# Graph attention, state-space mixer, relational layer and experts in one launch: mask transposes by transfer, small loads on another queue, and a new order of work

## The chip, the core and the metric

The kernel runs on one core of a Trainium2 chip. A core has five engines that run on their own and wait for each other through semaphores: PE (TensorE, matrix products and transposes into the PSUM banks), ACT (ScalarE), DVE (VectorE), POOL (GpSimd) and SP (SyncE, which issues transfers). Each engine executes its instructions in the order in which the program lists them; an instruction that waits holds up everything behind it on that engine. Transfers are issued from queues of SP, ACT and POOL and carried by 16 DMA engines that all queues share. SBUF is the working memory of 128 partitions, PSUM has eight banks of 128 x 512 floats, and the large tensors lie in the device's main memory (DRAM).

The metric is the device time of one launch in microseconds (us).

## The reference

`x` is 64 graphs of 256 nodes with 256 features in float32, `adj` the 64 adjacency matrices of 256 x 256 zeros and ones. Two layers follow one another, each of a graph part and a feed-forward part, each part with a residual and a layer norm (without scale) before it:

```python
x = x + _L0_gnn_ref(_layernorm(x), adj, W, a)                 # graph attention
x = x + _L0_ffn_ref(_layernorm(x), W_in, conv_w, ...)         # a Mamba-2 block
x = x + _L1_gnn_ref(_layernorm(x), ..., adj, weight, bias)    # relational layer
x = x + _L1_ffn_ref(_layernorm(x), gate_w, gate_b, w1, ...)   # 8 experts, top 1

def _L0_gnn_ref(h, adj, W, a):
    wh = einsum('bni,io->bno', h, W)
    s1, s2 = wh @ a[:Fout, 0], wh @ a[Fout:, 0]
    e = leaky_relu(s1[:, :, None] + s2[:, None, :], 0.2)
    e = where(adj > 0, e, NEG_BIG)
    return einsum('bmn,bno->bmo', softmax(e, axis=2), wh)

def _L1_gnn_ref(x, adj, relation, weight, bias):              # relation is adj
    masks = (relation[None] == rel_ids[:, None, None, None])  # 1..4
    h = einsum('rbnm,bmd->rbnd', masks, x)
    return einsum('rbnd,rdo->bno', h, weight) + bias
```

The Mamba-2 block projects to gates, values, B, C and dt, convolves over four positions, applies silu, mixes the 256 positions of a graph through a lower triangle of decays, gates, normalises by the root mean square and projects back (W_out, then W_lin). The expert layer sends each of the 16384 tokens to the expert with the largest gate, at most 2560 tokens to an expert, through relu(x w1 + b1) w2 + b2, scaled by the gate's probability.

## The kernel before

**Two passes.** The first pass (`first_pass`) goes through the 32 groups of two graphs (four tiles of 128 tokens each) and does everything up to the choice of an expert. It stores each token's row in a DRAM buffer (`x3d`) and its place in a list by experts (`slots`). The second pass (`second_pass`) goes through the blocks of 512 listed tokens (`wholes`) and of 128 (`quarters`): it gathers the rows, multiplies by the expert's weights and writes the rows out. Three whole blocks are already done within the first pass (`first_block`), to fill engines at its end, and the rows of the second pass's first block are fetched, normed and transposed there too (`lead`).

**The order of the first pass is planned.** Each function does not issue its instructions but registers steps with a planner (class `Plan`): engine, an assumed duration, what it reads and writes, an extra time until a result is visible (`late`), and the time of its transfer (`move`). `Plan.record` then simulates five engines and eight PSUM banks and issues the steps in the order in which they would begin; where several could begin at once, the one with the lower rank goes first. The rank is `PACE` times the group plus a due time from the tables `DUE` (a group's steps) and `LATE` (start and end). So the tables and the assumed durations set the order on every engine, and nothing else about the time: on the chip each engine follows its list and waits for what it needs. The second pass is not planned in this way; the framework orders its instructions.

**Start.** `prepare` loads and rearranges the weights. W_in goes to `win` (issued on ACT). `smaller` issues nine loads of small vectors, also from ACT: the convolution's weights `cw` and `cb` (halved on DVE afterwards), `aneg` (A_log), `dtb`, `dch` in two parts, `blin`, `brel`, `gb`. `centred` takes column means by a product with ones on PE (L516) and subtracts them on DVE (L522); `projected` transposes a matrix on PE (L533), copies it on ACT (L538) and multiplies it with the gate and logit columns (L544). The columns of W_in that give dt are copied on DVE out of `win` into the block `gq0` (L625). `aneg` becomes -exp(A_log) by an exponential on ACT (L638) and a product on DVE (L639), which wait for nothing but the load. `clear_slots` fills a tile on POOL and sends it over the `slots` list from ACT's queue (L721).

**A group.** `attention` loads x (L932) and the adjacency (`adji`, L935). ACT turns the adjacency into a bfloat16 mask `hide` (L947): 0 where an edge is, a large negative number elsewhere, three buffers. x is transposed on PE (L910) and copied by ACT (L915), multiplied with W (L871), and scaled by ACT into `wh` (L962). Then a chain begins: the logits `s2` are transposed on PE (L971), copied by ACT (`s2rows`, L973), written to DRAM and read back spread over all partitions by two transfers from SP (L975, L979); POOL adds the mask (`hm`, L983, two halves), ACT forms the other logits (`ev`, L989), DVE takes the row minima (L994), ACT the exponentials (L998), and PE transposes these (L1009) and multiplies them with `wh`. `scan` is the projection, the convolution (`y`, `xh`; DVE L1098, L1108) and the decays (four transfers `spread`, L1145; ACT `dm`, L1158 and L1164). `mix` multiplies decays and B-C products (DVE L1232, PE L1240 and L1244), gates and projects back. `relate` is the relational layer: products of the rows with the transposed mask `adjT`, then with the relation's weight. `choose`, once in two groups, finds experts and slots and scatters the token records (POOL L1436).

**The transposed masks.** In `mix`, for each of the two graphs of a group, PE transposes the four 128 x 128 blocks of `hide` with the bfloat16 identity `ident_b` into a PSUM bank (L1270), and ACT turns that into zeros and ones in `adjT` by a square with a scale and a bias (L1280), with a sum that is used to find adjacency values other than 0 and 1.

**Between the passes.** The second pass first fetches weights and token records, then gathers: `wholes.gather(0, None)` (rows of the first block, needed only as the residual there), then on POOL places and rows of `wholes` 1, `quarters` 0 and 1, then `quarters.norm(0)` on DVE.

Of the kernel before, what the change touches and what calls it, by code (L numbers as in the profile page):

```python
# [20 lines left out]
P = 128  # L21
# [15 lines left out]
    -26698, -26684, 16811, 5376, -1385, 22233, -9147, -5334, -6104, 16470, -4131, -12656,  # L37
    -16678, -3231, 6549, -17865, 6326, -26892, -31112, -17903, -11408, -796, -4422, -12203,
    -5594, 1406, -16327, -16058, -1084, -23798, -1397, -15584, 5401, -4898, -4435, 935, -15679,
    -4926, -36182, -30952, -7116, -5042, -13894, -12081, -3776, -29694, -776, -6149, -737,  # L40
    -14378, -1040, -15690, -8132, 2125, -13292, -19871, -13259, -19271, -17469, 3004, -3551,
    4598, 2717, -5807, -3518, -9626, -6760, -8973, -6760, -21580, -11090, -13187, -7075, -11614,
    8090, 12562, -15384, -25650, -16843, -17448, -16224, -33117, 17100, -11357, -1083, -673,
    -3047, -34625, -12261, -11942, 2714, -6609, 1789, 18383, -20000, 539, -3738, -33183, 333,
    14191, 6307, -9703, 30905, -7622, -19413, -14996, -28968, 116, 19317, 13445, 26060, -32817,
    248, -10405, 2927, -14690, 5944, -2080, -8721, 12774, 2204, -13729, 4024, -22409, -14504,
    5811, -7220, 1399, 13432, 6555, 4744, 7244, -13074, -17598, 12021, -2116, 1124, 383, 10928,
    4031, 2410, 19564, 20208, -4179, 14906, 17031, 1067, -9078, 28505, -6557, -15751, 31775,
    11208, -2943, -655, 18912, 7874, -12175, -12506, -31318, 19350, -32822, -27902, -1902,
    -2614, -22515, -11078, -32731, -7356, 9498, -25579, 6544, -6873, -12295, -8836, -15217,  # L50
    -101, -7100, 1503, -1212, -9384, -7250, 7131, 13184, 2367, 8234, -705, 2385, 15949, -10902,
    -6702, -11680, 4975, -8597, -19533, -14786, 2673, 6442, -7886, -3758, -14584, -18956, -2394,
    6472, -5117, -11835, -8654, 5355, -7098, 108, -26795, -19293, 8894, -21711, 8534, -22778,
    -5174, -16079, -18727, 6779, -14626, -18887, 15787, 204, 5445, -8225, -16055, 4780, 11196,
    -12432, -7396, 2489, -34797, 6092, -3614, -2035, -16485, -22244, -7928, 6163, -16171,
    -13402, 1393, 27308, -3299, 5434, 7440, -6001, 3226, -22066, 7952, -6124, -10687, 10110,
    -11601, -18846, 4084, -3318, -15991, -8790, -25459, 1833, -3473, -2961, -9107, -8293,
    -10502, -18974, -9710, -22513, -11406, -10557, -20206, -7421, -19897, -8699, -9302, -1570,
]
LATE = [  # L60
    -64053, -54702, -59145, -54915, -60062, -63895, -58481, -57817, -56638, -54542, -53887,
    -59553, -60544, -66295, -55138, -53590, -62371, -50547, -58476, -56411, -63929, -54771,
    -63020, -60249, -57757, -55870, -61971, -61584, -58713, -56315, -59515, -60412, -56997,
    -64050, -63593, -58710, -64327, -56974, -64548, -58677, -56261, -55764, -60770, -59294,
    -62214, -59216, -59275, -59000, -57674, -55104, -55629, -58061, -56012, -54911, -56448,
    -55347, -53242, -55651, -59000, -49001, -50233, -59769, -51850, -47995, -48427, -58143,
    -60315, -52513, -54188, -52953, -54782, -51621, -54327, -55185, -53707, -51746, -57084,
    -60544, -52244, -51134, -55346, -54169, -51215, -49728, -43803, -49582, -50567, -47711,
    -54575, -51840, -56142, -59770, -49885, 1346, -2673, -2320, -6355, -808, -6495, -5278,
    -5282, -4565, -4966, -834, -2200, -5069, -7821, -3201, -6160, -4309, -4527, -4910, -2257,  # L70
    -8341, -9201, -6505, -7591, -10768, -9145, -8325, -8954, 8280, 735, 3335, -7607, 7899, 6405,
    7444, -13853, 1045, -3011, 6416, -58, -9653, 9740, 2791, 9305, -3096, 1595, 7797, -2202,
    7339, -6677, 1395, 1189, 3316, 8270, 4320, 8345, 5395, -1209, 1024, 496, 4166, -5572, 10007,
    984, -7144, -1767, -9049, 430, 8168, 10157, 6125, 715, 2433, 5530, 2682, 9681, 4044, -3041,
    -2968, 5666, 3203, 7815, 2227, 4671, 4049, -972, 4835, -9096, 753, -943, -2244, 8804, -7176,
    9169, -3264, 14310, -351, -5008, 8557, -1420, 9011, 5402, 779, 9849, 8608, 3319, 8980, 5929,
    -754, -2251, 3474, -6957, 7127, 2274, 10247, -3481, 49, -3510, -403, -1726, 3946, 2006,
    -1802, 6377, 976, 1673, 5692, 3521, 6, -7831, -15890, 3058, 4170, -7076, 10709, 9000, 6424,
    5864, 2733, 2629, -4870, -702, -2673, 634, -1458, 1299, -687, 5733, -4310, 3394, -1918, 941,
    7852, -2182, 5064, -1684, 13692, 2798, 396, 8917, -2630, 8846, 9132, -2375, 11666, 11022,  # L80
    2337, 10279, 5111, 2075, -596, 5177, -3671, 3927, 3650, 11368, -4611, -3648, -135, -7000,
    2097, 4479, -1495, -2818, 6266, 3575, 372, 3192, -53, 1241, -9215, -13160, 8371, 1767,
    -8809, 9253, 10686, 2871, 6318, 5744, 6064, -7776, -3563, -2652,
# [59 lines left out]
class Plan:  # L143
# [6 lines left out]
    LEFT = 30  # L150

# [34 lines left out]
    def step(self, engine, us, go, reads, writes, late=0.0, port=0, move=0.0):  # L186
        k = self.k.get(self.due, 0)
        self.k[self.due] = k + 1
        due = (DUE if self.due == "group" else LATE)[k]
        step = Step(engine, us, go, self.g, self.TAIL[engine] + late, PACE * self.g + due,  # L190
# [128 lines left out]
def gnn_mamba_rgcn_moe(ctx: ExitStack, tc: tile.TileContext, a: dict, out: bass.AP):  # L319
# [33 lines left out]
    def row(ap):  # L353
        return ap.rearrange("(o d) -> o d", o=1)
# [33 lines left out]
    ident_b = const.tile([P, P], BF16, name="ident_b")  # L388
    nc.vector.tensor_copy(ident_b, ident)
# [92 lines left out]
    def first_pass(form, pass1):  # L482
# [80 lines left out]
        def smaller(s):  # L563

            def load(us, move, dst, src, home):
                s.step(ACT, us, lambda: nc.scalar.dma_start(out=dst, in_=src), [], [home], late=1.5, move=move)

            dskip = a["L0_ffn_D"].rearrange("(c q) -> q c", q=2)
            load(0.5, 0.2, cw, a["L0_ffn_conv_w"].rearrange("(c p) k -> p c k", p=P), s.fixed(cw))
            load(0.5, 0.2, cb, a["L0_ffn_conv_b"].rearrange("(c p) -> p c", p=P), s.fixed(cb))  # L570
            for half in (cw, cb):
                s.step(DVE, 0.1, lambda half=half: nc.vector.tensor_scalar(
                    half, half, 0.5, None, ALU.mult), [], [s.fixed(half)])
            load(0.5, 0.1, aneg, row(a["L0_ffn_A_log"]).broadcast_to([P, NH]), s.fixed(aneg))
            load(0.5, 0.1, dtb, row(a["L0_ffn_dt_bias"]).broadcast_to([P, NH]), s.fixed(dtb))
            for q in range(2):
                load(1.4, 0.1, dch[q * 64 : (q + 1) * 64, :], dskip[q : q + 1, :].broadcast_to([64, NCT]),
                     (s.fixed(dch), q))
            load(0.5, 0.5, blin[:, 0:D], row(a["L0_ffn_b_lin"]).broadcast_to([P, D]), (s.fixed(blin), "d"))
            load(0.5, 0.5, brel[:, 0:D], row(a["L1_gnn_bias"]).broadcast_to([P, D]), (s.fixed(brel), "d"))  # L580
            load(0.5, 0.1, gb, row(a["L1_ffn_gate_b"]).broadcast_to([P, E]), s.fixed(gb))

        def prepare(s):
# [36 lines left out]
            for i in range(2):  # L620
# [4 lines left out]
            s.step(DVE, 0.1, lambda: nc.vector.tensor_copy(gq0()[:, :, E + 1 :], win[:, :, DPROJ - NH :]),  # L625
                   [(win_, "dt")], [(two_, "q2")])
# [11 lines left out]
            s.step(ACT, 0.2, lambda: nc.scalar.activation(aneg, aneg, AF.Exp), [], [rate_])  # L638
# [78 lines left out]
        def clear_slots(s, homes):  # L717

            blank = s.tile("dm", [P, E * CAPP * 4 // P], bufs=4)
            s.step(POOL, 0.7, lambda: nc.gpsimd.memset(blank(), FAR), [], [blank])  # L720
            s.step(ACT, 0.5, lambda: nc.scalar.dma_start(  # L721
                out=slots.rearrange("(p j) w -> p (j w)", p=P), in_=blank()), [blank], homes, late=2.0, move=1.2)
# [457 lines left out]
        def mix(s, g, xe, entries, full, dt, gate, xh, bm, cm, dec):  # L1180
# [82 lines left out]
            adjT = []  # L1263
            for bi in range(2):
                ps, at = s.psum(BF16), s.tile("adjT", [P, 512], F32R, bufs=3)

                def turn(bi=bi, ps=ps):
                    for k in range(2):
                        for h in range(2):
                            nc.tensor.transpose(  # L1270
                                ps()[:, k * N + h * P : k * N + (h + 1) * P],
                                entries()[:, 2 * bi + h, k * P : (k + 1) * P],
                                ident_b,
                            )
# [349 lines left out]
    def second_pass(form, pass2):  # L1624
# [180 lines left out]
        for i in range(2):  # L1805
            quarters.fetch_weights(i)
# [76 lines left out]
```

## Time and profile before

| what | value |
|---|---|
| median of 3 runs | 2338.86 us (2333.72 to 2339.75) |
| profiled execution, its own time | 2332.68 us |
| its span, first to last instruction | 2331.0 us |
| granted PE clock, mean | 0.987 of full speed |
| instructions | 34861 |
| four mask transposes of a graph, count of instructions and busy time (L1270) | 256, 25.3 us |
| ACT's squares of the masks (L1280) | 64, 43.8 us |
| transfers of x and of adj, per group | 512 KB each, 5.3 and 4.6 us from issue to landing |
| transfers `spread`, four a group | 512 KB each, 4.0 us |

The profile is of one execution. Its span begins with the first instruction; the execution's own time is 1.7 us longer. Busy times of PE overlap, since products are pipelined: the busy time of a group of instructions can be more than what its absence would free. "PEld" is the loading of PE's weights, beside the products. Idle times are put down to what ended them ("<-"). Timeline lines show start, length, engine, line, operation, tiles written and read, and the idle time in front where there was some. In a table of stretches the columns are the stretch, its length, the busy time of PE, PEld, DVE, ACT and POOL with the number of instructions, the granted PE clock, the mean busy share of the DMA engines, and GB/s.

### The profile page before, as it was taken

Reading aid. Unit: us, or ns where it says so; the run is one execution under the profiler, and the core shown is the slowest. Engines: PE = TensorE matmul, PEld = TensorE weight load, DVE = VectorE, ACT = ScalarE, POOL = GpSimd, SP = SyncE. Lnnn points to the kernel's source line nnn. Section 1 sums busy time; section 2 is a strip of 40 time slices with the busy share of each in tenths; the row PEclk is TensorE's granted clock in tenths of the full one; section 3 lists DMA queues with packets and bytes.
Section 4 is the critical chain, followed back from the end, with each engine's and each line's share of the span. In section 5 each row is a group of like instructions: output and inputs, shape, how many; then the busy total and the mean of one; then the engine's idle time right before and its main releaser. Section 6 shows DMA issues by size and latency. Waiting matters only on the chain.

```text
span 2331.0 us, 34861 instructions
## 1 busy us (share of the span) xinstructions
PE 2232.1 (96%) x11079; PEld 1558.4 (67%) x11079; DVE 1757.0 (75%) x4396; ACT 1665.1 (71%) x3864; POOL 919.7 (39%) x994
## 2 busy tenths in 40 slices
PE   5999999999999999999999999999998999999996
PEld 4676766667676666766766667656665666666675
DVE  3899999999999998999998998799654434333342
ACT  3899999899999899999999988888632222222223
POOL 1233435354453445445354444533635222222221
PEclk7999999999999999999999999999999999999998
DMA  4333445444444445444444444424527333333336
GB/s 135 95 90 107 112 117 126 110 108 108 116 121 128 110 102 115 120 118 126 110 108 108 110 123 117 111 67 113 158 81 242 122 119 113 114 117 117 114 92 194
DMA packets 200022, 274.71 MB, mean 118 GB/s; under 512 B 28505, under 2 KB 165919, under 8 KB 199809
## 3 DMA queue, kind: packets, MB, share of 16 engines
q1 hardware_dynamic: 149968, 211.48, 28.9%
q0 software_dynamic: 46848, 58.91, 13.8%
q8 instruction: 93, 1.52, 0.3%
q10 hardware_dynamic: 2992, 1.81, 0.2%
q14 instruction: 121, 0.98, 0.2%
HBM read 187.70 MB, written 46.04 MB: 100 GB/s over the span
## 4 chain that ended last, share of the span: by engine, by line
PE 40%; issue 20%; ACT 12%; POOL 11%; DVE 10%; DMA 5%; SPq 0%; POOLq 0%; ACTq 0%; DVEq 0%
PE ps L871 26%; PE ps L1240 4%; POOL slots L1436 3%; POOL out_dram L477 3%; POOL xg L455 3%; ACT dm L1158 2%; DVE y L1098 2%; PE ps L910 2%; PE ps L1244 2%; PE ps L1543 1%; ACT dm L1164 1%; DMA x<-in_x_dram 1%; DVE dm L1232 1%; ACT xh L1256 1%; ACT xn L925 1%
## 5 line engine op out<-in xcount | busy, mean ns | idle before, releaser
L871 PE MATMUL ps<-xnT,win 128*128 128x512 f32 x1152 | 542.0, 597 | 4.8 <-ACT xnT L915 3.8
L1158 ACT ACTIVATE dm<-spread,cs 128x256 f32<-128x256 f32 (+1 forms) x1024 | 379.3, 452 | 22.6 <-PE ps L1244 22.6
L1098 DVE SCALAR_TENSOR_TENSOR y<-ps,cw,y 128x510 f32<-128x510 f32 (+2 forms) x480 | 351.5, 738 | 34.6 <-ACT y L1091 31.8
L871 PEld LDWEIGHTS ps<-xnT,win 128*128 128x128 f32 x1152 | 205.9, 190 | 171.6 <-issue 150.8
L1744 PE MATMUL ps<-w,hid 128*128 128x256 f32 x1184 | 263.3, 380 | 0.0
L871 PE MATMUL ps<-wf,gate 128*128 128x265 f32 x1024 | 250.8, 388 | 0.0
L1744 PEld LDWEIGHTS ps<-w,hid 128*128 128x128 f32 x1184 | 224.2, 191 | 37.0 <-issue 8.1
L1730 PE MATMUL ps<-xnT,w 128*128 128x512 f32 (+1 forms) x704 | 246.8, 509 | 1.5 <-ACT xnT L1711 1.5
L1232 DVE TENSOR_TENSOR dm<-dm,bc 128x1536 f32<-128x1536 f32 x128 | 225.2, 1760 | 2.5 <-ACT dm L1164 2.4
L871 PEld LDWEIGHTS ps<-wf,gate 128*128 128x128 f32 x1024 | 190.3, 190 | 45.2 <-issue 11.7
L1734 ACT ACTIVATE hid<-ps,b 128x512 f32<-128x512 f32 (+1 forms) x184 | 110.4, 604 | 129.4 <-PE ps L1730 126.1
L1730 PEld LDWEIGHTS ps<-xnT,w 128*128 128x128 f32 x704 | 120.6, 193 | 118.3 <-issue 111.0
L1164 ACT ACTIVATE dm<-dm 128x1536 f32<-128x1536 f32 x128 | 190.5, 1490 | 0.0
L1436 POOL DMA_INDIRECT slots<-meta,sl x128 | 153.8, 1201 | 50.6 <-issue 31.5
L1240 PE MATMUL ps<-dm,xdt 128*64 128x256 f32 x1024 | 169.4, 391 | 3.6 <-DVE xdt L1221 2.9
L889 DVE BATCH_NORM_STATS2 st<-x 128x6 f32<-128x256 f32 x384 | 155.2, 413 | 1.5 <-DMA x<-in_x_dram 1.3
L879 POOL TENSOR_SCALAR ve<-mv 128x4 f32<-128x4 f32 x96 | 36.6, 382 | 300.6 <-DVE mv L892 186.1
L1749 DVE SCALAR_TENSOR_TENSOR yv<-ps,meta,bp 128x256 f32<-128x256 f32 x50 | 24.2, 484 | 160.7 <-PE ps L1744 150.0
L871 PE MATMUL ps<-wrel,hr 128*128 128x265 f32 x512 | 136.1, 395 | 2.0 <-ACT hr L1349 0.5
L871 PE MATMUL ps<-wx,xT 128*128 128x292 f32 x512 | 134.9, 409 | 0.0
L1711 ACT COPY xnT<-ps 128x512 f32<-128x512 f32 (+1 forms) x48 | 21.4, 496 | 152.4 <-PE ps L1708 152.4
L871 PE MATMUL ps<-wh,eT 128*128 128x273 f32 x512 | 126.9, 395 | 0.5 <-ACT eT L1016 0.5
(311 smaller groups left out, 4845.1 us busy)
## 6 DMA issues: line engine op xcount, KB each, us to landing
spread<-sumd SPq DMA_DIRECT2D x128, 512.0 KB, 4.0
w<-in_L_ffn_w_dram SPq DMA_DIRECT2D x50, 1024.0 KB, 6.0
x<-blin POOLq DMA_DIRECT2D x32, 530.0 KB, 5.7
x<-brel POOLq DMA_DIRECT2D x32, 530.0 KB, 5.7
x<-in_x_dram SPq DMA_DIRECT2D x32, 512.0 KB, 5.3
adji<-in_adj_dram SPq DMA_DIRECT2D x32, 512.0 KB, 4.6
out_dram<-x SPq DMA_DIRECT2D x32, 512.0 KB, 3.0
x3d<-x SPq DMA_DIRECT2D x32, 512.0 KB, 6.1
```

The source lines that it names most:

```text
L455: nc.gpsimd.indirect_dma_start(out=dst, out_offset=None, in_=source, in_offset=bass.IndirectOffsetOnAxis(ap=col, axis=0),)
L871: nc.tensor.matmul(out_, lhsT=lhsT, rhs=rhs, start=(i == 0), stop=(i == len(pairs) - 1))
L889: s.step(DVE, 0.34, lambda j=j: nc.vector.bn_stats(sb()[:, j, :], src()[:, j, 0:D]), [(src, j)], [(sb, j)])
L1098: nc.vector.scalar_tensor_tensor(y3[:, :, d:], p3[:, :, : N - d], cw[:, c, k : k + 1], y3[:, :, d:], ALU.mult, ALU.add,)
L1158: nc.scalar.activation(dm()[:, q, bi, o : o + n], spr()[:, q, t1 - n : t1], AF.Relu, bias=cs()[:, 4 * h + j : 4 * h + j + 1], scale=-1.0,)
L1164: s.step(ACT, 1.38, lambda: nc.scalar.activation(dm(), dm(), AF.Exp, scale=-1.0), [], [dm])
L1232: s.step(DVE, 1.67, lambda dm=dm: nc.vector.tensor_mul(dm(), dm(), bc().unsqueeze(1).to_broadcast([P, 2, 2, N + P])), [bc], [dm], port=1)
L1240: nc.tensor.matmul(o, lhsT=xdt()[:, 2 * bi, h * 64 : (h + 1) * 64], rhs=dm()[:, q, bi, 0:N], start=True, stop=False,)
L1436: s.step(POOL, 1.1, lambda j=j: apart("slots", nc.gpsimd.indirect_dma_start(out=slots, out_offset=bass.IndirectOffsetOnAxis(ap=sl()[:, j : ...
L1730: nc.tensor.matmul(ps[:, :n], lhsT=w1[:, k, f * P : (f + 1) * P], rhs=turned[:, k, :], start=(k == 0), stop=(k == 1),)
L1734: nc.scalar.activation(hid[:, f, :], ps[:, :n], AF.Relu, bias=self.b1[i % 2][:, f : f + 1])
L1744: nc.tensor.matmul(ps[:, :D], lhsT=hid[:, f, j * P : (j + 1) * P], rhs=w2[:, f, :], start=(f == 0), stop=(f == NFT - 1),)
```

## The change

Five things:

1. The masks are transposed by a transfer from SP's queue, one for both graphs of a group (`dma_start_transpose`, from `hide` into a new tile `turned`, one buffer). ACT's square reads `turned` from SBUF in place of the PSUM bank. PE's two steps a group and `ident_b` are gone.
2. The nine small loads are issued from POOL's queue. The halvings of `cw` and `cb` and the exponential of `aneg` are registered after the weights `wx` and declared to read them, as is the transfer that clears the slots. The dt columns of W_in come by a load of their own into `gq0`.
3. In the second pass `wholes.gather(1, ...)` is written ahead of `wholes.gather(0, None)`.
4. The planner assumes PE steps 1.022 times as long (`SLOWER`).
5. `DUE` and `LATE` have new numbers throughout.

```diff
 class Plan:
     LEFT = 30
+    SLOWER = 1.022
     def step(self, engine, us, go, reads, writes, late=0.0, port=0, move=0.0):
...
         due = (DUE if self.due == "group" else LATE)[k]
+        us *= self.SLOWER if engine == PE else 1.0
...
-    ident_b = const.tile([P, P], BF16, name="ident_b")
-    nc.vector.tensor_copy(ident_b, ident)
...
             def load(us, move, dst, src, home):
-                s.step(ACT, us, lambda: nc.scalar.dma_start(out=dst, in_=src), [], [home], late=1.5, move=move)
+                s.step(POOL, us, lambda: nc.gpsimd.dma_start(out=dst, in_=src), [], [home], late=2.0, move=move)
...
-            load(0.5, 0.2, cw, a["L0_ffn_conv_w"].rearrange("(c p) k -> p c k", p=P), s.fixed(cw))
-            load(0.5, 0.2, cb, a["L0_ffn_conv_b"].rearrange("(c p) -> p c", p=P), s.fixed(cb))
-            for half in (cw, cb):
-                s.step(DVE, 0.1, lambda half=half: nc.vector.tensor_scalar(
-                    half, half, 0.5, None, ALU.mult), [], [s.fixed(half)])
+            load(1.1, 0.2, cw, a["L0_ffn_conv_w"].rearrange("(c p) k -> p c k", p=P), s.fixed(cw))
+            load(1.1, 0.2, cb, a["L0_ffn_conv_b"].rearrange("(c p) -> p c", p=P), s.fixed(cb))
...
-            s.step(DVE, 0.1, lambda: nc.vector.tensor_copy(gq0()[:, :, E + 1 :], win[:, :, DPROJ - NH :]),
-                   [(win_, "dt")], [(two_, "q2")])
+            load(0.3, lambda: gq0()[:, :, E + 1 :],
+                 a["L0_ffn_W_in"][:, DPROJ - NH :].rearrange("(k p) o -> p k o", p=P), (two_, "q2"))
...
-            s.step(ACT, 0.2, lambda: nc.scalar.activation(aneg, aneg, AF.Exp), [], [rate_])
+            for half in (cw, cb):
+                s.step(DVE, 0.1, lambda half=half: nc.vector.tensor_scalar(
+                    half, half, 0.5, None, ALU.mult), [wx_], [s.fixed(half)])
+            s.step(ACT, 0.2, lambda: nc.scalar.activation(aneg, aneg, AF.Exp), [wx_], [rate_])
...
             s.step(ACT, 0.5, lambda: nc.scalar.dma_start(
-                out=slots.rearrange("(p j) w -> p (j w)", p=P), in_=blank()), [blank], homes, late=2.0, move=1.2)
+                out=slots.rearrange("(p j) w -> p (j w)", p=P), in_=blank()), [blank, s.fixed(wx)], homes,
+                   late=2.0, move=1.2)
...
-            adjT = []
+            adjT, turned = [], s.tile("turned", [P, 2, 2, 2, P], BF16)
+            s.step(SP, 0.4, lambda: nc.sync.dma_start_transpose(
+                out=turned().rearrange("p b h k n -> p (b h k) n"),
+                in_=entries().rearrange("p j n -> p (j n)")), [entries], [turned], late=2.0, move=1.2)
             for bi in range(2):
-                ps, at = s.psum(BF16), s.tile("adjT", [P, 512], F32R, bufs=3)
-
-                def turn(bi=bi, ps=ps):
-                    for k in range(2):
-                        for h in range(2):
-                            nc.tensor.transpose(
-                                ps()[:, k * N + h * P : k * N + (h + 1) * P],
-                                entries()[:, 2 * bi + h, k * P : (k + 1) * P],
-                                ident_b,
-                            )
-
-                s.step(PE, 0.24, turn, [entries], [ps])
+                at = s.tile("adjT", [P, 512], F32R, bufs=3)
+
+                def square(bi=bi, at=at):
+                    out_ = at().rearrange("p (k h n) -> p k h n", k=2, h=2)
+                    in_ = turned()[:, bi].rearrange("p h k n -> p k h n")
...
+                        nc.scalar.activation(
+                            out_, in_, AF.Square, scale=-1.0 / NEG_BIG, bias=one,
+                            accum_out=tested[:, g, 1 + bi : 2 + bi])
+                s.step(ACT, 0.6 if full else 0.66, square, [turned], [at])
                 adjT.append(at)
...
+        wholes.gather(1, nc.gpsimd)
         wholes.gather(0, None)
-        for blocks, i in ((wholes, 1), (quarters, 0), (quarters, 1)):
-            blocks.gather(i, nc.gpsimd)
+        for i in range(2):
+            quarters.gather(i, nc.gpsimd)
```

Lines of the changed kernel are one or two higher than those of the kernel before: the attention transposes L1009 become L1011, for example, the squares L1280 become L1278, and the transposing transfer is L1266.

## The prediction

> **What bounds the kernel.** I read the busy time, then stretches with the granted clock, then who waits for whom, then the timeline where PE waits.
>
> ```profile
> PE 2232.1 (96%) x11079; PEld 1558.4 (67%) x11079; DVE 1757.0 (75%) x4396; ACT 1665.1 (71%) x3864; POOL 919.7 (39%) x994
> ```
>
> ```profile
> 16.00:23.00 7.00, 0.00 (x0) 0.00 (x0) 1.97 (x7) 1.49 (x2) 0.00 (x0) 0.70 0.64 189
> 23.00:30.00 7.00, 6.64 (x29) 6.31 (x29) 2.66 (x11) 2.08 (x5) 0.00 (x0) 0.50 1.01 347
> 30.00:38.00 8.00, 8.00 (x39) 7.86 (x40) 4.35 (x19) 1.92 (x4) 2.28 (x3) 0.50 0.12 19
> ...
> 400.00:600.00 200.00, 196.70 (x1074) 138.37 (x1074) 183.55 (x443) 182.68 (x437) 91.82 (x98) 1.00 0.46 114
> ```
>
> The columns are stretch, length, busy PE, PEld, DVE, ACT, POOL, clock, DMA share. In the steady stretch (four groups) PE is 98% busy, DVE and ACT 91 to 92%: PE is the bound, the two others 4 us a group behind it. At the start PE does nothing for 7 us and then works 15 us at half clock.
>
> ```profile
> PE ps L1009 <- ACT ev L998: 17.1, 23, 5.6
> ...
> PE ps L533 <- DVE gate L522: 8.2, 1, 8.2
> ```
>
> ```profile
> DVE aneg L639 <- ACT aneg L638: 10.7, 1, 10.7
> ```
>
> ```profile
> ACT L638 <- DMA cw<-in_L_ffn_conv_w_dram: 19.5, 1, 19.5
> ```
>
> PE's two largest waits. The one at L533 runs back through DVE, which stands at aneg (L639) with the centring of the weights (L522) queued behind it, to ACT, whose exponential follows the loads that it issues.
>
> ```profile
> 516.80 0.40 PE L1270 MATMUL ps<-ident_b,hide 128*128 128x128 bf16 x4
> 517.03 0.61 PE L910 MATMUL ps<-ident,x 128*128 128x128 f32 x4
> ...
> 533.93 0.27 PE L971 MATMUL ps<-ident,wh 128*128 128x128 f32 x1
> ...
> 551.43 1.04 PE L1009 MATMUL ps<-ident,ev 128*128 128x128 f32 x8
> ```
>
> ```profile
> 540.37 2.29 POOL L983 TENSOR_TENSOR hm<-hide,s 128x512 f32<-128x512 bf16 x2
> ```
>
> Four mask transposes hold PE 517.03 - 516.80 = 0.23 us (the group's 25.3 us of busy time overlaps its neighbours). From the s2 transpose (L971) to the attention transposes (L1009) a chain over two transfers, POOL, DVE and ACT takes 17.5 us.
>
> ```profile
> 1791.19 0.41 DVE L461 TENSOR_SCALAR xn<-xg,meta 128x256 f32<-128x256 f32 x1 [18.67 <-DMA xg<-x3d,place]
> ...
> 1792.64 2.30 PE L1708 MATMUL ps<-ident,xn 128*128 128x128 f32 x8 [7.72 <-DVE xn L461]
> ```
>
> Between the passes PE waits 7.7 us. The DVE instruction in front is one row (x1): the quarters' norm ahead, with the second block's norms (x4) queued behind it.
>
> **The change, part by part.**
>
> *Masks.* Removed from PE: 64 steps of four transposes, 64 x 0.23 = 14.7 us, and 64 uses of a PSUM bank. Where PE is the bound all of it is on the path; I take 14.7, bounds 0 (PE waits in the same place anyway) and 25.3 (the busy time). ACT's square now reads SBUF: 688 ns from PSUM against 632 (L1104, SBUF source), 64 x 0.056 = 3.6 us less on an engine off the path: 0.
>
> Added on SP: 32 transposing transfers of 256 KB. No row shows one. Issue on SP: 0.34 us (spread) to 2.0 (the longest single issues). Landing: 2.0 us (cm<-bm, 64 KB from SBUF to SBUF) to 8.0 (four such). Taken: 1 and 4, nearest the 512 KB loads at 4.0 to 4.6. Queued behind it on SP are the fourth spread, the next adji, s2d and s2. That spread itself waits for ACT's decays (SP waited 385.8 us at L1145, 45 times, 8.6 each), which hides the issue; without that cover each late us goes into s2 and from there to PE. ACT waits in order at the square, with hr, wh, hide and the decays behind it, and PE behind hr. In the order that the changed kernel builds, 35 ACT instructions stand between the last square of one group and the first of the next (more in every second group); their durations in this trace add up to 19.8 us, and since ACT's instructions overlap (15.3 us of summed durations took 12.5 in the chain above, factor 0.81) that is 16 us. 8.0 fits twice: 0. The transfers load the DMA engines by 0.26 of some 5.8 MB a group (4.5%), or, as 1024 packets of the mean 80 ns, by 5 us of 50; PE's waits for x were 6.0 us in 24 groups, so 0 to 3 us; taken 1.
>
> The Trainium skill speaks against the edit: "VectorE: DVE Perf Modes", section "Rules for kernel authors", wants TensorE for a 128x128 transpose where PSUM will do, and its section "The three transpose paths" puts 390 ns for it there and 1309 through DMA. PE's row here is 58 ns each in a stream. Eight blocks one after another at the page's figure would be an estimated 10.5 us, inside the 16, and the sum would stay.
>
> *Start.* The nine small loads go to POOL: 9 x 1.13 (L701's issue) = 10.2 us, in a POOL that waited 28.2 us for L701. aneg's exponential and the halvings come behind wx, so the centring no longer stands behind them, and the dt columns come by a load of their own. The slowest small load took 7.3 us (cw); cb is issued sixth, near 10 us, and lands by 17, while DVE reaches it only after wx, near 18: covered; each us beyond delays wrel and PE one for one. (PE starts at 7.6 with win's arrival as before; win, w0 and q are 4.5 + 1.4 + 2.0 us of its rows, W_out's transposes of 1.1 move in among them: 16.6, plus 1.1 for wx.) The 8.2 us at L533 go, W_out's 1.1 being only moved. Returned: the clearing of slots, a 2.0 us issue on ACT, now stands ahead of the copies for wrel: 0 to 2, taken 1. PE's 14.64 busy us at clock 0.50 (23 to 38) would be 7.3 shorter at full clock if the idle stretch no longer precedes them; copies on ACT lie between its steps, so 0 to 7.3, taken 4.3. Sum: 8.2 - 1 + 4.3 = 11.5.
>
> "TensorE: Matmul & The Clock Gate", section "What's actually happening", says the clock halves after an idle window of some 3.4 us and returns after as long a busy one. The rows agree (7 us idle, then 0.50), though here half clock outlasted 14 us of near-full work; by the page alone all 7.3 would go, an estimated 3 us more than I take.
>
> *Rows gathered first.* In the order built, POOL still issues the gathers for the first block, then the second's, then the quarters', as before, and DVE still has the quarters' norm in front. The 7.7 us stay: 0, bounds 0 and 4 (one place in a queue of four gathers at 0.97).
>
> *Plan.* PE steps 2.2% longer and new due times move nearly every instruction, but not their number. Summing durations per instruction in the orders built, PE's work for two groups falls from 95.7 to 94.7, the transposes alone; before took 100.2. What differs is the room for the s2 chain: PE work between the s2 and attention transposes is 17.2 us before and 13.1 and 13.4 after. ACT's work from s2rows to the second exponential, all the first four transposes need, is 14.3 and 13.8 summed, x 0.81 = 11.6 and 11.2, plus 0.78 until s2rows starts: 12.4 and 12.0, inside 13.1. The transfers and POOL need 0.78 + 5.66 + 1.15 until half of hm, then two DVE minima and an exponential (1.5): 9.1. So 0, with 0.7 us to spare. Bounds: half of PE's 40 idle us between 60 and 1700 gained (-20), or the old 17.5 us kept (4.4 x 30 groups = +132).
>
> Sum: 14.7 + 11.5 - 1 = 25 us. From the profiled execution's 2332.7 (span 2331.0 and 1.7 around it): 2307.7. It ran 6.2 us under the median of 2338.9, so 2313.9, say 2314.
>
> **Rivals.**
> - *The new order's s2 chain is too short (slower).* Place: PE at the attention transposes (L1011 after), waiting for ACT's exponentials. For it: the room shrinks by 4 us, this is already PE's largest wait, and DVE and ACT have only 4 us a group free. Against: the sums above fit, and POOL no longer has indirect writes between the halves of hm. Each us late costs some 30; from 0.84 it eats the gain, from 1.1 it is slower. At 2 us: 2314 + 60 = 2374.
> - *The transposing transfer lands late (slower).* ACT stands at the square. Decides from 16 us; at 19 us 3 us in 16 to 32 groups: 2314 + 48 to 96, some 2386. Against: twice my upper bound.
> - *Only the start gains.* PE, freed of the transposes, waits 0.46 us a group more for DVE or ACT: 2314 + 14.7 = 2329.
> - *Nothing in sum.* New waits of 0.7 to 0.8 us a group: 2336. That the gathers don't move is already in the sum.
>
> **How the numbers follow.** Forecast 0.66, start alone 0.08, nothing 0.08, short chain 0.14, late transfer 0.04. A difference under 0.3% (7 us: 2332 to 2346) can't be told from no change. Faster takes the first two and a little of the third, 0.75; same 0.08; slower 0.17. The forecast's own range: best 14.7 + 15.5 + 15 of idle = 45, 2294; worst the start at 7.2 and half the transposes, 2325. For 8 in 10 I reach up to 2346 and leave out the slower cases and a little below.
>
> **What would show it.** Right: no L1270 on PE; no wait at L533 over 1 us; clock near 1.00 between 16 and 38 us; pairs of groups near 99.2 us; the transposing transfer landing under 8 us with no ACT wait at L1278; the 7.7 us at L1708 still there. Wrong: a PE wait at L1011 near 1 us in every group, ACT idle at L1278, DVE standing at cb or cw at the start.

## The result, and the profile after

The changed kernel takes 2342.69 us (median of 18 runs, 2338.75 to 2352.97), the kernel before 2336.44 (18 runs, 2329.0 to 2341.0): 1.0027 times as long, 95% interval 1.0019 to 1.0035. 2314 was forecast. The profiled executions differ by 10.5 us of span (2341.5 against 2331.0).

The first part of the changed kernel's page:

```profile
PE 2230.4 (95%) x10823; PEld 1541.2 (66%) x10823; DVE 1801.8 (77%) x4394; ACT 1661.4 (71%) x3864; POOL 932.5 (40%) x1003
```

PE has 256 instructions less and is hardly less busy. DVE is 45 us busier with two instructions less: its instructions have become longer. Stretches of the changed kernel, columns as before:

```profile
16.00:23.00 7.00, 6.66 (x48) 6.32 (x47) 4.75 (x25) 1.70 (x6) 0.98 (x2) 0.90 0.88 290
23.00:30.00 7.00, 7.00 (x32) 6.04 (x31) 4.73 (x16) 2.16 (x5) 1.40 (x3) 0.86 0.69 228
...
400.00:600.00 200.00, 193.88 (x1031) 134.12 (x1030) 188.59 (x435) 179.19 (x429) 92.53 (x97) 1.00 0.49 115
```

The idle 7 us of the start are gone and the half clock mostly (0.90 and 0.86 up to 30 us, where it was 0.70 and 0.50), and the first attention transposes begin at 43.2 us, not 56.5. In the steady stretch PE is busy 193.9 us of 200, not 196.7, and DVE 188.6, not 183.6. PE's waits in the changed kernel (in total, times, longest):

```profile
PE ps L1011 <- ACT ev L1000: 19.9, 34, 9.8
PE ps L912 <- ACT xn L927: 11.3, 11, 3.4
...
PE ps L873 <- DVE oh L1409: 7.2, 11, 4.3
PE ps L1730 <- issue: 6.8, 1, 6.8
PE ps L873 <- DVE run L1413: 5.7, 11, 0.5
```

The wait at L533 is gone. At L1011 the longest is the first group's 9.8 us; between 400 and 1200 us none is over 0.7, so the room for the s2 chain suffices. New are the waits for oh and run, and that for xn has grown (3.0 us in 3 before). They lead back to one place, which the timelines of GpSimd, VectorE and ScalarE show in turn (start, duration, instruction):

```profile
769.34 1.35 POOL L922 DMA_DIRECT2D x<-brel  x1
770.22 1.78 POOL L1260 TENSOR_TENSOR xh<-xh 128x512 f32<-128x512 f32 x1
```

```profile
769.57 2.49 DVE L1050 TENSOR_TENSOR dv<-x,rs 128x32 f32<-128x32 f32 x1
771.98 0.21 DVE L1402 TENSOR_TENSOR lg<-lg,lmx 128x64 f32<-128x64 f32 x1
```

```profile
772.23 0.26 ACT L1403 ACTIVATE ex<-lg 128x64 f32<-128x64 f32 x1 [2.27 <-DVE lg L1402]
```

VectorE's dv, otherwise 0.2 to 0.4 us, lasts 2.49 and ends with GpSimd's addition of squares (xh, L1260); the logits (lg) stand behind it, and ScalarE stands 2.27 us for them, once in each pair of groups of the steady part. By form, before and after (instructions | busy us, mean ns):

```profile
L1048 DVE TENSOR_TENSOR dv<-x,rs 128x32 f32<-128x32 f32 x32 | 9.2, 287 | 6.7 <-POOL rs L880 6.7
L1063 DVE SCALAR_TENSOR_TENSOR dt<-dv,q 128x32 f32<-128x32 f32 x32 | 6.0, 187 | 0.4
```

```profile
L1050 DVE TENSOR_TENSOR dv<-x,rs 128x32 f32<-128x32 f32 x32 | 28.7, 896 | 4.0 <-POOL rs L882 4.0
L1065 DVE SCALAR_TENSOR_TENSOR dt<-dv,q 128x32 f32<-128x32 f32 x32 | 13.5, 422 | 0.1
```

Summed over VectorE's instructions more than 0.25 us above the median of their line and form, such stalls are some 27 us before and 67 after; beside the additions of squares some 18 (21 times) and 61 (55 times).

The ledger of the two profiled executions: some 13 us won by the first attention transposes; 101.42 us a pair of groups in place of 100.33, so that the lead is used up by groups 22 and 23 (one ends 6.6 us later than before, the other 6.4 earlier); 9 lost in the last eight groups; 1.4 in the second pass.

### The profile page after: what moved, and what is told of

Same layout as the page of the kernel before. It is cut to its first block, busy times and chain, and to the rows that moved or that the text cites. A ratio compares the mean times of both kernels' runs of the same rounds, so it can differ in the third digit from the quotient of the medians.

```text
span 2341.5 us, 34426 instructions
## 1 busy us (share of the span) xinstructions
PE 2230.4 (95%) x10823; PEld 1541.2 (66%) x10823; DVE 1801.8 (77%) x4394; ACT 1661.4 (71%) x3864; POOL 932.5 (40%) x1003
## 5 line engine op out<-in xcount | busy, mean ns | idle before, releaser
L1100 DVE SCALAR_TENSOR_TENSOR y<-ps,cw,y 128x506 f32<-128x506 f32 (+2 forms) x480 | 354.2, 741 | 28.2 <-ACT y L1093 25.5
L1730 PE MATMUL ps<-xnT,w 128*128 128x512 f32 (+1 forms) x704 | 246.6, 509 | 1.4 <-ACT xnT L1711 1.4
L1234 DVE TENSOR_TENSOR dm<-dm,bc 128x1536 f32<-128x1536 f32 x128 | 235.1, 1836 | 6.7 <-ACT dm L1166 6.0
L1730 PEld LDWEIGHTS ps<-xnT,w 128*128 128x128 f32 x704 | 120.4, 193 | 118.3 <-issue 110.7
L881 POOL TENSOR_SCALAR ve<-mv 128x4 f32<-128x4 f32 x96 | 50.8, 529 | 320.8 <-DVE mv L894 319.4
L891 DVE BATCH_NORM_STATS2 st<-x 128x6 f32<-128x256 f32 x384 | 150.1, 416 | 10.3 <-DMA x<-in_x_dram 10.0
L873 PE MATMUL ps<-wx,xT 128*128 128x292 f32 x512 | 143.1, 415 | 0.1
L873 PE MATMUL ps<-wh,eT 128*128 128x273 f32 x512 | 132.5, 402 | 4.2 <-ACT eT L1018 4.2
L873 PE MATMUL ps<-wrel,hr 128*128 128x265 f32 x512 | 130.6, 392 | 3.8 <-ACT hr L1349 3.2
L1093 ACT ACTIVATE y<-ps,cb,cw 128x512 f32<-128x512 f32 x160 | 123.6, 772 | 7.5 <-PE ps L873 7.4
```

The costliest lines, as they stand in the source:

```text
L873: nc.tensor.matmul(out_, lhsT=lhsT, rhs=rhs, start=(i == 0), stop=(i == len(pairs) - 1))
L891: s.step(DVE, 0.34, lambda j=j: nc.vector.bn_stats(sb()[:, j, :], src()[:, j, 0:D]), [(src, j)], [(sb, j)])
L1093: s.step(ACT, 0.66, lambda: nc.scalar.activation(y(), ps(), AF.Identity, scale=cw[:, c, 3:4], bias=cb[:, c : c + 1]), [ps, s.fixed(cw), s. ...
L1100: nc.vector.scalar_tensor_tensor(y3[:, :, d:], p3[:, :, : N - d], cw[:, c, k : k + 1], y3[:, :, d:], ALU.mult, ALU.add,)
L1234: s.step(DVE, 1.67, lambda dm=dm: nc.vector.tensor_mul(dm(), dm(), bc().unsqueeze(1).to_broadcast([P, 2, 2, N + P])), [bc], [dm], port=1)
L1730: nc.tensor.matmul(ps[:, :n], lhsT=w1[:, k, f * P : (f + 1) * P], rhs=turned[:, k, :], start=(k == 0), stop=(k == 1),)
```

## The experiments

Every experiment replays a recorded order of instructions step by step, so that a part of the change can be made without its new plan; the list of the order makes the line numbers some 430 higher (L1009 becomes L1443 to L1448). The pace is the time between the ends of groups 5 and 23 (the fourth addition x, L1358) over nine pairs. Where the values change, so does the routing, and with it the second pass (603 to 678 us in these runs), and only the first pass is compared. Ratios are to runs of the kernel before made beside the run (their medians are 2335.2 to 2338.0). The last two columns are of one profiled execution each, and starts differ: in the six runs of the order of before with the new start, PE's transposes and all of GpSimd's additions the first group ends at 178.0 to 183.0 us.

| Run | Median us | Ratio to before (95%) | Pace | First pass ends |
|---|---|---|---|---|
| before | 2336.4 | | 100.33 | 1721.4 |
| changed kernel | 2342.7 | 1.0019 to 1.0035 | 101.42 | 1730.5 |
| start_only | 2321.7 | 0.9926 to 0.9954 | 100.55 | 1717.4 |
| masks_only | 2337.9 | 1.0004 to 1.0022 | 100.38 | 1726.9 |
| start_and_masks | 2326.7 | 0.9949 to 0.9975 | 100.52 | 1720.4 |
| new_order_PE_turns | 2353.4 | 1.0067 to 1.0094 | 102.07 | 1738.0 |
| after_no_adds | values change | | 99.14 | 1700.3 |
| start_no_adds | values change | | 100.27 | 1704.7 |
| after_bc_first | 2331.9 | 0.9974 to 0.9992 | 99.97 | 1718.2 |
| no_turns | values change | | 100.23 | 1722.3 |
| after_apart | 2346.5 | 1.0025 to 1.0057 | 101.45 | 1731.5 |
| after_dt_ahead | 2328.7 | 0.9962 to 0.9981 | 99.94 | 1717.8 |
| start_old_gather | 2324.2 | 0.9928 to 0.9958 | 100.49 | 1711.9 |
| s2_early, dve_less, act_less | values change | | 100.34, 100.35, 100.29 | |
| start_pool | 2301.1 | 0.9843 to 0.9877 | 98.58 | 1691.8 |
| start_masks_pool | 2295.0 | 0.9805 to 0.9842 | 97.34 | 1687.0 |
| pool_masks_from_2 | 2296.3 | 0.9805 to 0.9840 | 97.30 | 1685.6 |

**The change in parts.** The edits are parts of the diff above; start_only has the gathers of the changed kernel, start_old_gather undoes the last part of the diff there.

> The kernel before with the new start alone: small loads on GpSimd's queue, the dt columns by a load, the halvings and aneg's exponential behind wx, the clearing of slots behind wx. Every other instruction stands in the order of before, replayed step by step, with PE's mask transposes. The theory that the start works and something later takes it back: 11 to 13 us under before (about 2324), as the changed kernel's trace shows at its first attention transposes (43.2 against 56.5 us) and at 70 us. The theory that the early lead is eaten in the steady stretch whatever the order (DVE or ACT sets the pace there): within 4 us of before.

> The kernel before with the masks turned by one transposing transfer a group and nothing else: the old start, and PE, DVE, ACT, POOL and SP in the order of before, with PE's 64 transposing steps left out and the transfer put into SP's order some 16 us ahead of the first square. If my prediction's step holds (all of the transposes are on the path): 14.7 - 1 = 13.7 us under before, about 2323. The theory that the transfer spoils what it saves (1.8 us of issue on SP, 1000 packets of 256 bytes a group, s2 and spread land later): no faster than before, up to 10 us slower. The theory that DVE and ACT hold the pace as soon as PE is relieved: 0 to 5 us under before.

> Both parts, new start and masks by transfer, with the order of before replayed: the change without its new plan. If the new order of instructions is what cost the time, this is faster than both kernels: 24 to 27 us under before, about 2311, and some 31 us under the changed kernel. If the transfers are to blame, it is no faster than the start alone (about 2324) or slower. If DVE and ACT hold the pace, about 2320 to 2324.

> The changed kernel in its own order, replayed, with the masks turned on PE again (64 steps of four transposes put into PE's order 2.5 us ahead of each square, a fourth buffer for hide in the place of the turned tile). If the new order of instructions is to blame and PE's work is on the path: 5 to 15 us slower than the changed kernel (2348 to 2357). If the transfers are to blame: faster than the changed kernel by 10 us or more, about 2330. If PE is no longer what holds the pace in this order: within 3 us of the changed kernel.

> The run with the new start alone (2321.7) with the row gathers issued in the order of before. My prediction's step says that the order of the gathers is worth nothing (0, bounds 0 to 4): 2321 to 2323. If it is worth what the second passes of the two kernels differ by (609.6 us after the first pass with the old order, 606.4 with the new): 3 us slower, about 2325.

The start is worth 14 us, the order of the gathers nothing that can be told. In the order of before, turning the masks by transfer saves nothing: 2.3 us more alone, 5 more with the new start. In the new order it saves 10.7 (2353.4 - 2342.7). The new order costs 31.7 with PE's transposes, which are set into it by hand (2353.4 - 2321.7), and 16 with the transfer (2342.7 - 2326.7). So two steps of the prediction fail: the transposes, and the plan.

**The plan.** Two runs without GpSimd's additions (the first diff; the third addition likewise), and one that keeps all the work and changes 11 places of GpSimd's queue (the second, with the lines of the changed kernel):

```diff
-                s.step(POOL, 1.3, lambda c0=c0: nc.gpsimd.tensor_add(
-                    sq()[:, c0 + 1, :], sq()[:, c0 + 1, :], sq()[:, c0, :]), [(xh, c0)], [(xh, c0 + 1)], port=1)
+                s.step(POOL, 1.3, lambda: None, [(xh, c0)], [(xh, c0 + 1)], port=1)
```

```diff
 rs L882
+bc L1205
+xh L1260
 x<-brel L922
-xh L1260
-bc L1205
```

> The changed kernel in its own order, without GpSimd's three additions of squares a group (so the norm's sum holds one chunk of four; the routing, and with it the number of blocks in the second pass, can shift a little). In the changed kernel's trace VectorE stands 63.5 us in 55 instructions while one of these additions runs; in the trace of before 17.9 us in 20. The theory that these stalls are what the new order costs: 15 to 30 us under the changed kernel, 2313 to 2328, and much more gained here than without the additions in the order of before. The theory that the stalls lie beside other waits: within 6 us of the changed kernel.

> Control: the order of before with the new start (2321.7 us measured), again without GpSimd's three additions of squares a group (the norm's sum holds one chunk of four). Its trace has 18.3 us of VectorE stalls under these additions. The theory that the stalls are what separates the two orders: 0 to 8 us under 2321.7. If the additions' work itself is on the path in any order, it gains as much as the changed kernel does without them.

> The changed kernel with all its work, in its own order but for GpSimd's queue in 11 pairs of groups: the causal selection (bc) and then the addition of squares stand ahead of the issue of the bias transfer (brel), not behind it, so that VectorE's dv and the logits behind it run before the addition begins. The theory of the stalls: dv takes 0.2 us in place of 2.5, ScalarE's exponential of the logits no longer waits 2.3 us a pair, and the kernel is 8 to 20 us faster than the changed one (2323 to 2335). The theory that the order costs in another place: within 4 us of the changed kernel.

Without the additions the first pass ends 30.2 us earlier in the new order and 12.6 in the old one, and the pace falls by 2.3 and 0.3 us a pair. The difference of 17.6 is more than the 10.1 us by which the new order's first pass is behind the old one's (1730.5 against 1720.4, both with the transfer): the additions, with the stalls beside them, carry it, though the two runs differ in how the masks are turned too. The changed places alone bring 10.8 us; dv takes 0.27 us at the median there, and ScalarE waits 1.7 us for the logits between 400 and 1200 us, not 19.8 (the changed kernel, then after_bc_first: total, times, longest):

```profile
ACT ex L1403 <- DVE lg L1402: 19.8, 8, 2.5
```

```profile
ACT ex L1837 <- DVE lg L1836: 1.7, 6, 0.3
```

Two moves in VectorE's queue were to take further stalls away (after_apart has both, after_dt_ahead the first alone):

```diff
+dt L1065
 xh L1110
-dt L1065
```

```diff
 y L1100
+dm L1234
 y L1100
-dm L1234
```

> The run with the causal selection ahead (2331.9), and two more stalls taken away by moving one VectorE instruction each: in every second group dt goes ahead of the product xh, into a stretch in which VectorE waits for ScalarE anyway (8 groups), and the decay product dm goes ahead of one convolution tap that reads PSUM (10 groups), so that it begins before the addition of squares does. All the work is done. The theory of the stalls: 1.07 + 0.7 to 1.1 us a pair of VectorE's standing less, 5 to 15 us faster than 2331.9, some 2317 to 2327. If only the stall in front of the logits counted: within 3 us of 2331.9.

> One of the two moves of the run that turned out 14 us slower than expected: dt ahead of the product xh in 8 groups, the decay product dm where the changed kernel has it. If dm ahead of the tap did the harm (its 1.75 us stand before the tap that ScalarE's tanh waits for: ScalarE waited 18.9 us in 800 there, against 5.7): at or a little under 2331.9, 2326 to 2332. If dt did it (it stands before the product that ends the chunk): 2340 or more.

after_apart came out some 14 us slower than after_bc_first, though VectorE stood 8 us less beside the additions. ScalarE's waits over 400 to 1200 us in it and in after_bc_first show why:

```profile
ACT xh L1540 <- DVE y L1534: 18.9, 15, 1.9
```

```profile
ACT xh L1540 <- DVE y L1534: 5.7, 10, 0.7
```

dm now stands ahead of the tap that ScalarE's tanh (xh L1540) needs. dt alone brings 3 us, which is at the edge of the noise; with it 14 of the new order's 16 us are back. A stall costs what waits behind it, not its length.

**The transposes.**

> The kernel before in its own order and with its old start, with the masks not turned at all: neither TensorE's transposes nor the transfer; the squares read the masks as they lie (so the second sums are taken along the other axis of the mask, and the routing and the second pass's blocks can shift). It stands beside the run with the transfer alone (2337.9). If the transfer costs what TensorE saves: 12 to 16 us under before, about 2321. If TensorE doesn't hold the pace in the order of before, so that its 14.7 us only become longer waits: 0 to 5 us under the run with the transfer, 2333 to 2338.

Without any turning (and with a fourth buffer for hide) the first pass ends 0.8 us after that of before, at a pace of 100.23 against 100.33. So it isn't the transfer that eats the gain; PE's work was hardly on the path. The timeline of PE in masks_only and, for the next microseconds, its stretches show the saved time come back as a wait:

```profile
599.34 1.88 PE L1305 MATMUL ps<-xnT,win 128*128 128x512 f32 x4
603.06 0.33 PE L1443 MATMUL ps<-ident,ev 128*128 128x128 f32 x1 [1.84 <-ACT ev L1432]
```

```profile
602.00:604.00 2.00, 0.78 (x5) 0.59 (x6) 2.00 (x4) 2.00 (x8) 0.00 (x0) 1.00 1.03 374
604.00:606.00 2.00, 2.00 (x4) 0.76 (x4) 2.00 (x7) 2.00 (x5) 0.00 (x0) 0.60 0.76 267
606.00:608.00 2.00, 2.00 (x7) 1.31 (x6) 2.00 (x4) 1.23 (x3) 1.10 (x2) 0.55 0.67 258
```

Once a pair PE waits 1.84 us at the attention transposes, where it waited 0.88 before: the difference is about the pair's four steps of 0.23. And behind some of these waits the granted clock is 0.50 for 3.4 us. The half clock doesn't hide the gain: the five pairs of masks_only without it take 99.5 to 99.8 us, and the five pairs of before in which PE does not wait 0.9 us or more for x take 99.7 to 99.9. That is some 0.1 us of the 0.92 removed. Which engine holds the exponentials back? Three runs on start_only make one suspect lighter each, in the order s2_early, dve_less, act_less:

```diff
-                out=s2(), in_=line.broadcast_to([P, 4 * P])), ...
+                out=s2(), in_=x[0, 0:2, :].rearrange("(o h) d -> o (h d)", o=1).broadcast_to([P, 4 * P])), ...
-                    s.step(DVE, 0.65, tap, [ps], [y])
+                    s.step(DVE, 0.65, tap if c or k else lambda: None, [ps], [y])
-                    accum_out=vr()[:, o + j : o + j + 1]), ...
+                    accum_out=vr()[:, o + j : o + j + 1]) if j < 3 else None, ...
```

> What holds the pace in the order of before, if not TensorE? The run with the new start alone, in which the spreading of the s2 line reads 512 values of the input x in the place of the line just stored, so that it no longer waits for the store's landing (the attention's logits, the routing and the second pass's blocks differ; the first pass's pace is what is read: 100.5 us a pair of groups). If the s2 chain holds the pace: the chain is some 2 us shorter, TensorE's wait at the attention transposes (8.4 us in 800) goes, 99.5 us a pair or less. If ScalarE's and VectorE's queues hold it: 100.2 to 100.6.

> The run with the new start alone without one of the fifteen convolution taps a group on VectorE (the last tap of the first channel chunk is left out, so the values, the routing and the second pass's blocks differ; the pace of the first pass is read). 0.74 us a group less on VectorE: if VectorE's queue holds the pace, up to 1.5 us a pair less, 99.0 to 99.5; if the s2 chain or ScalarE does, 100.2 to 100.6.

> The run with the new start alone without one of ScalarE's four squares of x a group (the row variances for the routing are all taken from the first row; the routing and the second pass's blocks differ; the pace of the first pass is read, 100.5 us a pair). 0.7 us a group less on ScalarE. TensorE's transposes, the early s2 line and VectorE's tap were worth 0.1, 0.2 and 0.2 us a pair. If ScalarE's queue holds the pace in the order of before: 99.0 to 99.8 us a pair. If no single engine does (the order itself, with waits going from one engine to the next): 100.2 to 100.6.

None of them does (0.2 to 0.3 us a pair). What is left is the engine that is busy 39% of the time. GpSimd's timeline in the trace of before, at the same place of a pair, and VectorE's:

```profile
582.28 1.30 POOL L1436 DMA_INDIRECT slots<-meta,sl  x1 [0.73 <-DVE sl L1433]
...
588.19 2.15 POOL L1436 DMA_INDIRECT slots<-meta,sl  x1 [0.30 <-issue]
590.64 0.97 POOL L1436 DMA_INDIRECT slots<-meta,sl  x1 [0.30 <-issue]
591.92 0.98 POOL L1436 DMA_INDIRECT slots<-meta,sl  x1 [0.30 <-issue]
592.89 1.09 POOL L1309 TENSOR_TENSOR r2r<-r,mhalf 128x4 f32<-128x4 f32 x1
593.93 1.18 POOL L983 TENSOR_TENSOR hm<-hide,s 128x512 f32<-128x512 bf16 x1
595.28 1.21 POOL L1436 DMA_INDIRECT slots<-meta,sl  x1 [0.17 <-issue]
596.51 1.18 POOL L983 TENSOR_TENSOR hm<-hide,s 128x512 f32<-128x512 bf16 x1
```

```profile
582.63 0.16 DVE L1307 TENSOR_SCALAR r<-ps 128x4 f32<-128x4 f32 x1
...
594.01 0.89 DVE L1312 SCALAR_TENSOR_TENSOR x<-ps,r2r,x 128x265 f32<-128x265 f32 x2 [2.56 <-POOL r2r L1309]
```

r is ready at 582.8, and r2r begins at 592.9, behind seven writes of slots, which nothing reads before 1581 us (the blocks done at the end of the first pass). VectorE waits 2.56 us for it, the minima behind that for hm, ScalarE for the minima, PE for ScalarE. The edit is on GpSimd's queue alone (r2r and hm move together, so their shares are not told apart):

```diff
 slots 1
+r2r
 slots 2, 3, 4
+hm, hm
 slots 5, 6, 7
-r2r, hm
 slots 8
-hm
```

> The run with the new start alone (2321.7) with one more edit, on GpSimd's queue only: in each pair of groups the power r2r stands behind the first of the eight indirect writes of slots, and the two additions hm behind the fourth, in place of r2r and the first hm behind the seventh and the second hm behind the eighth. In the traces r is ready 0.4 us after the first write begins, r2r begins 10 us later, VectorE waits 2.6 us a pair for it, ScalarE 2.1 for the minima behind it, TensorE 0.9 for the exponentials. If GpSimd's queue holds the pace in the order of before: 99.3 to 99.8 us a pair in place of 100.5, 8 to 14 us in all, 2308 to 2314. If the pace is held elsewhere: within 3 us of 2321.7.

> The same edit of GpSimd's queue with new start and masks by transfer (2326.7). There TensorE waits 1.84 us a pair at the attention transposes, and in 5 of 10 pairs its clock is halved for some 3.3 us behind that wait. If GpSimd's queue is what turned TensorE's saved 14.7 us into waits: the wait and the halved clock go, 98.3 to 99.2 us a pair, 20 to 28 us under 2326.7, 2299 to 2307, and faster than every other run. If not: within 3 us of 2326.7.

> The run of new start, transfer and reordered GpSimd queue (2295.0), with the masks of the first two groups turned on TensorE and by transfer from the third on. In the runs with the transfer the first attention transposes begin 7.5 us later than in the runs without (51.8 against 44.3 us). If the transfer of the first groups is what delays the start: first attention transposes near 44 us and 4 to 8 us under 2295.0, 2287 to 2291. If the transfer costs that time elsewhere: within 2 us of 2295.0.

20.6 us for start_pool, more than expected: the pace falls by 2 us a pair. There the transfer pays, 6.1 us (2301.1 to 2295.0) and 1.24 us a pair; start_masks_pool too is faster than expected (2299 to 2307), and the result is 1.6 to 2.0% faster than before. The GpSimd timeline of start_pool has the first hm 8 us behind the first write, where it was 11.7:

```profile
567.33 1.30 POOL L1875 DMA_INDIRECT slots<-meta,sl  x1 [0.73 <-DVE sl L1872]
568.65 1.77 POOL L1748 TENSOR_TENSOR r2r<-r,mhalf 128x4 f32<-128x4 f32 x1
...
575.40 2.32 POOL L1422 TENSOR_TENSOR hm<-hide,s 128x512 f32<-128x512 bf16 x2
```

The last run missed: with PE turning the first two groups the start stays 6 us behind that of start_pool (end of the first group), as with the transfer from the start (7.6). In both of these runs the clock is 0.64 and 0.50 between 16 and 30 us (start_pool: 1.00 and 0.76), with waits of 1.9 to 2.3 us for one early load in place of 1.0. But neither the transfer nor that wait decides: start_and_masks, with the transfer, waits 2.8 us for the same load and has 1.00 and 0.76, and start_only, without it, waits 1.3 us and has 0.69 and 0.50. What sets the clock there stays open.

## Why the prediction was wrong

- **Start, -11.5: right.** The run alone gives 14 us less (10.7 to 17.3 by its interval). L533's wait is gone, the issue for clearing slots took 0.37 us, not 1, and the clock came back in part: how much differs between runs with the same start, as the last experiment shows.
- **Rows gathered first, 0: nothing contradicts it** (ratios 0.9943 and 0.9940, the same within the noise). The 7.7 us at L1708 did not stay in that place; 6.8 us at L1730 are there now, with nothing that the profile shows as their cause.
- **The transfer's own cost, 1: small, as taken.** Between no_turns and masks_only the pace differs by 0.15 us a pair, some 2.4 us in all; PE's waits for x are 7.5 us in 9 waits, where they were 6.0 in 6. The transfer's rows in the changed kernel (min/median/max ns):

```profile
L1278 ACT ACTIVATE adjT<-turned,tri x64: 704/712/781, 34.5 to 1679.7; 128x512 fp32r<-128x512 bf16 x64
...
L1266 SPq DMA_TRANSPOSE turned<-hide x32: 1252/1812/3126, 31.3 to 1647.5; - x32
```

 The issue took 1.8 us at the median (taken: 1), the square 712 ns and not the 632 that I had from another row, and ScalarE waited for the data once, 0.3 us. There the square began 3.2 us after the issue did (34.5 and 31.3 us), near the 4 taken and far below the 10.5 estimated for eight blocks one after another.
- **Masks, "Where PE is the bound all of it is on the path; I take 14.7": this step failed.** PE was 98% busy, but its largest wait in the steady stretch, for ScalarE, led through VectorE to GpSimd's queue: reordering that queue alone brought 20.6 us. I had stopped at PE's share. In the order of before the 14.7 us are worth nothing; in the new order, where VectorE waits 2.4 us for r2r between 400 and 1200 us and not 20.3, they are worth 10.7; with GpSimd's queue mended 6.1.
- **Plan, "So 0, with 0.7 us to spare": this step failed by 16 us** (31.7 without the transfer). The room for the s2 chain was right: waits at L1011 of 0.3 us on the mean. But I summed durations "per instruction in the orders built" as if an instruction took what it took in another order. The new order puts two-operand instructions of VectorE beside GpSimd's additions, and they stand. The Trainium skill's page "SBUF — State Buffer", section "Who interferes with whom", has the rule: a VectorE instruction with two inputs in SBUF contends with a GpSimd instruction that reads SBUF, by an exclusive lock. The rows agree: dv, dt and dm stand (2.49, 1.25 and 2.90 us in place of 0.19, 0.18 and 1.75), while the taps y, which read PSUM, keep their 0.74 us beside the same additions. The planner does hold such steps apart: a step with `port` set does not begin, in the simulation, while a step of the other engine with `port=1` runs. But only the order reaches the chip, and there dv and the addition met. That 2342.7 lies under the 2346 up to which the prediction reached is luck: the two failed steps lost more than the start won.
- **The rivals.** The short s2 chain, named as the slower one, did not come. "Nothing in sum" came nearest (2336). Its new waits of 0.7 to 0.8 us a group came, and it named no cause for them: ScalarE and PE wait behind stalls of VectorE, and in the order of before behind GpSimd's queue.

## What to carry to other kernels

The engine with the largest busy share need not hold the pace: follow its steady wait back through every queue, and ask at the last one what stands ahead that nobody needs yet. Where a change reorders, durations are not constants: list which instructions share a port and see in the trace, not in the plan, which now run side by side. And replay the old order to separate an edit from a new plan: here that led from +0.27% to -1.8%.

## What had not been expected of the hardware

- The stall of dv begins 0.65 us before the addition's record, while GpSimd's issue of a transfer is still running, and lasts 2.49 us; issues with no addition behind them stalled nothing (25 dm at 1.73 to 1.76 us, their usual time).
- 13 of the 31 waits of 1.83 to 1.85 us in masks_only, start_and_masks and no_turns were followed by some 3.4 us at half clock, 1.7 us lost each; none of the 15 waits of 0.7 to 1.62 us in the steady part of before was (in the changed kernel one such stretch followed waits of 0.7, 0.5 and 0.2 us close together). The Trainium skill, "TensorE: Matmul & The Clock Gate", section "HAM oscillation — how this bites in real kernels", warns of idle gaps over some 3.4 us; here a gap of half that was enough, and the measurement decides.
